# Output projection weights loaded at the start, and part of the first block's output projection moved into the last attention head

## The chip, the cores and the metric

The kernel runs on one core of a Trainium2 chip. The metric is device microseconds of one execution, the median of several runs. The core has a matrix engine (TensorE, PE in the profile, with its weight loads as PEld), VectorE (DVE), ScalarE (ACT), GpSimd (POOL) and the sync engine (SP), which here only issues transfers. 16 DMA engines move data. SBUF is the on-chip memory of 128 partitions, PSUM the memory that matrix products are written to.

## The reference

In short form, one layer with x of shape (1, 2048, 256): attention over 16 heads of 128, then a mixture of 8 experts of which 2 are used for each token. Weights of the attention come as codes and block scales (32 rows share a scale), and w = codes × scales.

```python
def attn(x):                                   # x: layernorm of the input
    q, k, v = (mxfp4(x, w) + b for w, b in ...)          # 256 -> 2048
    scores = einsum("bqhd,bkhd->bhqk", q, k) / sqrt(128)
    out = einsum("bhqk,bkhd->bqhd", softmax(scores), v)  # 2048 x 2048 per head
    return mxfp4(out, wo_codes, wo_scales) + bo          # 2048 -> 256
def ffn(x):                                    # x: layernorm of the sum so far
    top2 weights = normalised top 2 of softmax(x @ Wr)
    y_e = (silu(x @ Wg[e]) * (x @ Wu[e])) @ Wd[e]        # e = 0..7, I = 176
    return sum over e of weight_e * y_e
x = x + layernorm(attn(layernorm(x)))
x = x + layernorm(ffn(layernorm(x)))
```

## The kernel before

**Numbers.** For accuracy most products are made in two parts: a value is split into a high half in fp16 (or fp32r) and a low half that is the rest. Scores take three matmuls per tile (high×high, high×low, low×high), and so do the products with v.

**Stages.** A lead-in normalises x, transposes it (`xnT`) and makes the first projections. The main loop has 16 heads × 16 tiles of 128 queries, counted by g = 16 h + t, and two steps more (`NS` = 256, g = 256 and 257) that only finish softmax work. The tail does the output projection of four blocks of 512 queries, the two layernorms, the router and the experts.

**One step g of the main loop**, in the order in which each engine gets its instructions: scores of the first half of the keys into PSUM (12 matmuls for both halves, L492 to L496) and their maximum on DVE (L497); the second half of the low part of tile g−2 (`pl`, DVE, L537); a part of the products with v (`pv_unit`, L563); the high part of tile g−1 (`ph`, ACT, L522); scores of the second half, then exponentials on ACT (`p`, L508); the first half of `pl` of tile g−1. `ph` and `pl` are written as [queries, keys], and the products with v need [keys, queries]: each is transposed by a transfer on the sync queue (`pth` L525, `ptl` L543), two per step, 512 in all. The products with v run 13 units (6.5 steps) behind. Projections of the next head's q and k, and of v for the next pair of heads, fill the step (`fill`, L591); in head 15 only q is left, at t = 0, 4 and 8.

**Slots.** One pool of SBUF tiles (`kqv`, tag "x", `NX` = 21 slots of 4 KB per partition) holds `kT`, `v`, `ph`, `pl`, `wo`, the staging of weights, `oi` and other tiles of the tail. A new tile takes the slot that has been free for longest in the order of the program, and its writer waits until the last reader of the old tile is done; for `ph` and `pl` that includes the transposing transfer.

**Output of a head.** When a block of 512 queries of a head is done, ACT evicts the sum (`t32`, L578), POOL splits it (L579, L580) and stores it to DRAM (`ot_d`, L583). The output projection later loads it back in tiles `oi` of 4 heads × 256 queries, 512 KB each, on the sync queue (`load_oi`, L698). `op_mm(b, half, js)` adds up the products of 256 queries of block b with heads 4j to 4j+3, 16 matmuls a j, into one PSUM tile.

**Output weights.** `wo` is stored in DRAM as codes and scales. In head 14 three of its eight parts are loaded on POOL's queue (`load_wo_part`, L620), in head 15 five (`load_wo`, L637): each has four broadcast loads of scales on ACT's queue, L641, and one of codes on the sync queue, L646. POOL multiplies them (`dequant_wo`, L654, 128x512, eight times). With `wo` there, the row of biases is made (`bias_row`, `bias_row2`, L656 to L670), at t = 12 and 13 of head 15. `late(t)` (L718) also loads the gate weights (`wg`, t = 7 to 11), splits them (t = 10 to 13), and loads the first `oi` tiles (t = 9 and 11 to 14; three more at g = NS).

**Tail.** L1078 onwards: the last `pv` units (9, of which the first belongs to the last but one block), the output projection of block 0 (`op_pass(0, 0)`, `op_pass(0, 1)`, 128 matmuls), layernorms, router, and that of block 1 between them; then 44 steps of gate, up and down products with the rest in between.

The order of each engine's instructions is that of the program: nothing is rescheduled (`manual_schedule`). PSUM tiles of the projections have one buffer a tag ("pj", "pv"), scores have three ("s").

Of the kernel before, what the change touches and what calls it, by code (L numbers as in the profile page):

```python
# [37 lines left out]
def sandwich(  # L38
# [183 lines left out]
    def proj_qk(which, h, b, tag="pj", wide=None):  # L222
# [12 lines left out]
        t = kq_tile(which, h, b)  # L235
# [41 lines left out]

    with tc.tile_pool(name="start", bufs=4) as st:
# [18 lines left out]
        for i, (which, codes, scales) in enumerate(  # L297
            (("k", wk_codes, wk_scales), ("q", wq_codes, wq_scales), ("v", wv_codes, wv_scales))
        ):
            nc.gpsimd.dma_start(out=sc8[:, i], in_=scales[:, 0:256])  # L300
            cd = st.tile([128, 2, 256], F32, name="cd0", bufs=3)
            nc.sync.dma_start(
                out=cd, in_=codes.rearrange("(kc p) n -> p kc n", p=128)[:, :, 0:256]
            )
            cds[which] = (i, cd)
        nc.gpsimd.memset(one3, 1.0)
# [284 lines left out]
    def fill(h, t):  # L591
# [3 lines left out]
        if t in QK:  # L595
# [19 lines left out]
    wo = []  # L615
    so = wo_scales.rearrange("(h b) n -> b h n", b=4)
    co = wo_codes.rearrange("(h p) n -> p h n", p=128)
    wo_raw = {}

    def load_wo_part(j, part):  # L620
        hs = slice(2 * j, 2 * j + 2)
        if part == 0:
            wo_raw[j] = (
                stage.tile([128, 2, D], F32, name="wos", tag="st_s"),
                stage.tile([128, 2, D], F32, name="woc", tag="st_c"),
            )
        sc, cd = wo_raw[j]
        if part < 2:
            for b in (2 * part, 2 * part + 1):
                nc.gpsimd.dma_start(  # L630
                    out=sc[32 * b : 32 * b + 32],
                    in_=so[b : b + 1, hs].to_broadcast([32, 2, D]),
                )
        else:
            nc.gpsimd.dma_start(out=cd, in_=co[:, hs])

    def load_wo(j, pool, tags, bufs):  # L637
        hs = slice(2 * j, 2 * j + 2)
        sc = pool.tile([128, 2, D], F32, name="wos", tag=tags[0], bufs=bufs)
        for b in range(4):  # L640
            nc.scalar.dma_start(  # L641
                out=sc[32 * b : 32 * b + 32],
                in_=so[b : b + 1, hs].to_broadcast([32, 2, D]),
            )
        cd = pool.tile([128, 2, D], F32, name="woc", tag=tags[1], bufs=bufs)
        nc.sync.dma_start(out=cd, in_=co[:, hs])  # L646
        wo_raw[j] = (sc, cd)

    def dequant_wo(j):
        sc, cd = wo_raw.pop(j)  # L650
        if j % 4 == 0:
            wo.append(kqv.tile([128, 8, D], BF, name="wo", tag="x", bufs=NX))
        hs = slice(2 * (j % 4), 2 * (j % 4) + 2)
        nc.gpsimd.tensor_tensor(wo[j // 4][:, hs], cd, sc, ALU.mult)  # L654
# [12 lines left out]
    def bias_row2(b3):  # L667
        pb2 = psA.tile([128, 512], F32, name="pb2", tag="pj")
        nc.tensor.matmul(pb2[:, :D], one3, b3, start=True, stop=True)
        nc.vector.tensor_tensor(crow, pb2[:, :D], crow, ALU.add)  # L670
# [27 lines left out]
    def load_oi(b, half, j, tag="x"):  # L698
# [3 lines left out]
        nc.sync.dma_start(  # L702
# [9 lines left out]
    gw, crow = None, None  # L712
    gst = {}

    WO_LOAD = (0, 2, 4, 6, 8)
    WG_LOAD = (7, 9, 10, 11)

    def late(t):  # L718
        nonlocal gw, crow
        if t in WO_LOAD:  # L720
            load_wo(3 + WO_LOAD.index(t), kqv, ("x", "x"), NX)
        if t - 1 in WO_LOAD:
            dequant_wo(3 + WO_LOAD.index(t - 1))
        if t == 13:
            bias_row2(gst.pop("b3"))
        if t == 12:
            gst["b3"] = bias_row()
        if t == 9:
# [3 lines left out]
            crow = rp.tile([128, D], F32)  # L732
            nc.sync.dma_start(out=crow, in_=bo.partition_broadcast(128))
        if 10 <= t < 14:
            split_gu(gw, t - 10, gst.pop(t - 10), True)
        if t in WG_LOAD:
            i = WG_LOAD.index(t)
            gst[i] = load_gu(wg, i, kqv, "x", NX)
        if t == 9:
            load_oi(0, 1, 0, "x")  # L740
        if 11 <= t < 15:
            load_oi(0, 0, t - 11)

    X1 = {}
    XV = x.rearrange("b (c p t) d -> p (b c) t d", p=128, t=4)
# [3 lines left out]
    for g in range(NS + 2):  # L749
# [8 lines left out]
        if g == NS:  # L758
            load_oi(0, 1, 1)
            load_oi(0, 1, 2)  # L760
            load_oi(0, 1, 3)
# [35 lines left out]
        if h == NH - 2 and t in (8, 12):  # L797
            dequant_wo(t // 4 - 2)
        if h == NH - 1 and t == 0:
            dequant_wo(2)  # L800
        if h == NH - 2 and t >= 4 and t % 4 < 3:
            load_wo_part(t // 4 - 1, t % 4)
        if h == NH - 1:
            late(t)
        if g == NS:
            X1[0] = kqv.tile([128, 4, D], F32, name="x1_0", tag="x", bufs=NX)
            nc.sync.dma_start(out=X1[0], in_=XV[:, 0])
    UEND = 2 * (NS + 2)


    AT, MV, XT, CT = {}, {}, {}, {}

    OPS = {}

    def aux_psum(shape, dtype, name, tag):
        if tag == "s":
            return psS.tile(shape, dtype, name=name + "_s", tag="s", bufs=3)
        return psA.tile(shape, dtype, name=name, tag=tag)

    def op_mm(b, half, js, tag="pj"):  # L820
        if js[0] == 0:
            if half == 0:
                AT[b] = kqv.tile([128, 4, D], F32, name="at", tag="x", bufs=NX)
                MV[b] = small.tile([128, 4, 2], F32, name="mv")
            OPS[(b, half)] = aux_psum([128, 2, D], F32, "op", tag)
        ps = OPS[(b, half)]
        for j in js:
            oi = OIN.pop((b, half, j))
            for t in range(2):
                for hh in range(4):  # L830
                    for hl in range(2):
                        nc.tensor.matmul(  # L832
                            ps[:, t], oi[:, hh, hl, bass.ts(t, 128)],
                            wo[j // 2][:, 4 * (j % 2) + hh, :],
                            start=(j == 0 and t == 0 and hh == 0 and hl == 0),
                            stop=(j == 3 and t == 1 and hh == 3 and hl == 1),
                        )
        if js[-1] == 3:
            at = AT[b]
            tt = slice(2 * half, 2 * half + 2)  # L840
            nc.vector.scalar_tensor_tensor(
                at[:, tt], ps, sig[:, 0, 2:3],
                crow.unsqueeze(1).to_broadcast([128, 2, D]), ALU.mult, ALU.add,
            )
            stats(at, MV[b], 2 * half, 2 * half + 2)

    def op_pass(b, half, tag="pj"):
        op_mm(b, half, (0, 1, 2, 3), tag)

    def stats(src, mv, t0, t1):  # L850
        bs = small.tile([128, 4, 6], F32, name="bs")
        for t in range(t0, t1):
            nc.vector.bn_stats(bs[:, t], src[:, t, :])
        for t in range(t0, t1):
            nc.vector.bn_aggr(mv[:, t, :], bs[:, t])

    def norm(dst, src, mv, r):
        for t in range(4):
# [379 lines left out]
```

## Time and profile before

| what | value |
|---|---|
| runs | 1836.58 to 1838.99 us, median of 4: 1838.6 us |
| profiled execution | 1837.48 us, span 1835.7 us, granted clock 0.995 |
| TensorE busy | 1777.7 us, 97% of the span |
| DVE, ACT, POOL busy | 1626.8, 1369.8, 956.0 us |
| one step of the main loop | 5.86 to 5.90 us in heads 1 to 13, 5.94 in head 14, 6.17 in head 15 |
| end of the scores of head 15 | about 1544 us after the span's start |
| first gate product | 1602.58 us |

A step's time is the distance between the first `ph` of a head and that of the next, over 16. "Busy" counts an engine's own work. "Idle before" is the time in which an engine had nothing to do before an instruction, and the releaser is what it waited for last. The granted clock is the share of full speed at which TensorE was allowed to run. A DMA issue has a duration on its queue and, later, a landing.

### The profile page before, as it was taken

The page shows a single profiled execution, that of the slowest core. Times are in us where ns is not written, and L with a number is a line of the kernel's source. Part 1 is how long each engine was busy: PE and PEld are TensorE (multiplying, and loading weights), DVE is VectorE, ACT ScalarE, POOL GpSimd, SP SyncE. Part 2 cuts the span into 40 slices and gives each one's busy share as a digit, 9 for nine tenths or more (in the row PEclk, how much of TensorE's full clock was granted, in tenths as well). Part 3 has the DMA queues.
Part 4 walks back from the last instruction along what each step waited for, and adds up shares of the span by engine and source line. Part 5 has one row for each costly group of instructions (what it writes and reads, how often), then busy time and mean ns, then how long its engine had stood idle before and what let it go on. Part 6 is the DMA issues. An engine that isn't in the chain of part 4 may idle for free. (4 is left out here: it accounts for less than half of the span.)

```text
span 1835.7 us, 25522 instructions
## 1 busy us (share of the span) xinstructions
PE 1777.7 (97%) x8890; PEld 933.4 (51%) x8890; DVE 1626.8 (89%) x2267; ACT 1369.8 (75%) x1730; POOL 956.0 (52%) x929
## 2 busy tenths in 40 slices
PE   6899999999999999999999999999999988899998
PEld 4344444444444444444444444444444434688887
DVE  7999999999999999999999999999999886468566
ACT  5888888888888888888888888888888776222232
POOL 3366566555655565556565656565546433323232
PEclk9999999999999999999999999999999999999999
DMA  2999999999999999999999999999999999921000
GB/s 84 178 203 201 197 206 196 198 199 199 197 198 202 199 196 200 204 204 188 205 201 199 201 194 206 195 195 202 193 189 208 210 216 240 345 87 35 1 12 24
DMA packets 1091505, 330.71 MB, mean 180 GB/s; under 512 B 1070048, under 2 KB 1078064, under 8 KB 1091376
## 3 DMA queue, kind: packets, MB, share of 16 engines
q1 hardware_dynamic: 1078688, 298.14, 88.4%
q0 software_dynamic: 10544, 29.40, 5.9%
q10 hardware_dynamic: 2144, 1.54, 0.3%
q8 instruction: 70, 1.15, 0.2%
q14 instruction: 59, 0.48, 0.1%
HBM read 41.68 MB, written 18.87 MB: 33 GB/s over the span
## 5 line engine op out<-in xcount | busy, mean ns | idle before, releaser
L508 ACT ACTIVATE p<-s,m,ssc 128x1024 f32<-128x1024 f32 x512 | 612.1, 1199 | 183.7 <-DVE m L501 174.4
L537 DVE SCALAR_TENSOR_TENSOR pl<-p,m,ph 128x1024 f16<-128x1024 f32 x512 | 723.6, 1413 | 12.8 <-ACT ph L522 12.7
L497 DVE TENSOR_REDUCE m<-s 128x1 f32<-128x1024 f32 x512 | 622.1, 1215 | 28.0 <-PE s L496 26.2
L522 ACT ACTIVATE ph<-p,m 128x2048 f16<-128x2048 f32 x256 | 512.9, 2003 | 53.5 <-ACT t L274 14.5
L563 PE MATMUL pv<-pth,v 128*128 128x512 f16 x2048 | 507.8, 381 | 14.0 <-ACT p L508 5.3
L563 PEld LDWEIGHTS <-v 128*128 128x128 f16 x3072 | 301.0, 98 | 382.5 <-issue 11.7
L492 PE MATMUL s<-kT,qT 128*128 128x512 f16 x1024 | 388.7, 380 | 11.6 <-ACT p L508 10.7
L493 PE MATMUL s<-kT,qT 128*128 128x512 f16 x1024 | 388.5, 379 | 0.0
L496 PE MATMUL s<-kT,qT 128*128 128x512 f16 x1024 | 305.0, 379 | 0.0
L563 PE MATMUL pv<-ptl,v 128*128 128x512 f16 x1024 | 251.9, 379 | 0.0
L244 POOL CAST qT<-t 128x512 f16<-128x512 f32 x63 | 80.0, 1270 | 234.3 <-ACT t L243 234.3
L275 POOL CAST v<-t 128x256 f16<-128x256 f32 (+1 forms) x105 | 43.1, 410 | 255.4 <-ACT t L274 255.4
L276 POOL TENSOR_TENSOR v<-t,v 128x256 f16<-128x256 f32 (+1 forms) x105 | 163.8, 1560 | 8.5
L493 PEld LDWEIGHTS <-qT 128*128 128x128 f16 x1024 | 100.2, 98 | 125.2 <-issue 19.7
L496 PEld LDWEIGHTS <-qT 128*128 128x128 f16 x1024 | 100.3, 98 | 121.2 <-issue 0.6
L492 PEld LDWEIGHTS <-qT 128*128 128x128 f16 x1024 | 100.2, 98 | 110.0 <-issue 1.4
L993 POOL TENSOR_TENSOR hh<-sg,hh 128x512 fp32r<-128x512 f32 x42 | 55.1, 1312 | 143.3 <-ACT hh L992 108.7
L992 ACT CAST hh<-sg 128x512 fp32r<-128x512 f32 (+1 forms) x45 | 27.5, 611 | 107.1 <-DVE sg L1004 107.0
L580 POOL TENSOR_TENSOR o<-t,o 128x512 f16<-128x512 f32 x63 | 98.9, 1570 | 5.2
L508 ACT ACTIVATION_READ_ACCUMULATOR p<-s,m,ssc 128x1 f32 x512 | 99.0, 193 | 0.0
L244 POOL CAST kT<-t 128x512 f16<-128x512 f32 x60 | 65.5, 1091 | 55.9 <-ACT t L243 48.3
L245 POOL TENSOR_TENSOR kT<-t,kT 128x512 f16<-128x512 f32 x60 | 88.0, 1467 | 5.1
(186 smaller groups left out, 1831.7 us busy)
## 6 DMA issues: line engine op xcount, KB each, us to landing
oi<-ot_d SPq DMA_DIRECT2D x32, 512.0 KB, 5.5
ot_d<-o POOLq DMA_DIRECT2D x63, 256.0 KB, 4.5
pth<-ph SPq DMA_TRANSPOSE x256, 5.0
ptl<-pl SPq DMA_TRANSPOSE x256, 5.2
xt<-in_L_attn_x SPq DMA_DIRECT2D x4, 512.0 KB, 4.6
x<-in_L_attn_x SPq DMA_DIRECT2D x4, 512.0 KB, 6.2
st_s<-in_L_attn_wv_scales POOLq DMA_DIRECT2D x28, 64.0 KB, 4.2
st_c<-in_L_attn_wv_codes POOLq DMA_DIRECT2D x14, 128.0 KB, 4.3
```

The lines of the kernel that those rows point to most:

```text
L244: nc.gpsimd.tensor_copy(t[:, 0, :], t32)
L245: nc.gpsimd.tensor_tensor(t[:, 1, :], t32, t[:, 0, :], ALU.subtract)
L276: nc.gpsimd.tensor_tensor(v[:, 1, sl, :], t32, v[:, 0, sl, :], ALU.subtract)
L492: nc.tensor.matmul(s[:, j, :], q[:, 0, qc], k[:, 0, :], start=True, stop=False)
L493: nc.tensor.matmul(s[:, j, :], q[:, 0, qc], k[:, 1, :], start=False, stop=False)
L496: nc.tensor.matmul(s[:, j, :], q[:, 1, qc], k[:, 0, :], start=False, stop=True)
L497: nc.vector.tensor_reduce(m[:, half : half + 1], s, AX.XY, ALU.max)
L508: nc.scalar.activation(p[:, bass.ts(i, 1024)], s, AF.Exp, bias=m[:, 2:3], scale=ssc[:, 0:1], accum_out=m[:, 3 + i : 4 + i],)
L522: nc.scalar.activation(ph, p, AF.Copy, scale=m[:, 6:7])
L537: nc.vector.scalar_tensor_tensor(pl[:, cs], p[:, cs], m[:, 6:7], ph[:, cs], ALU.mult, ALU.subtract)
L563: nc.tensor.matmul(ps, V[(h // 2, c // 4)][:, i % 2, c % 4, dc], d[:, :, c, :], start=(n == 0), stop=(n == 47),)
L580: nc.gpsimd.tensor_tensor(o[:, :, 1, :], halves(t32), o[:, :, 0, :], ALU.subtract)
```

## The change

All codes and scales of `wo` are loaded in the lead-in, on the sync queue after the codes of the first projections, into eight slots of the pool: four loads of 512 KB and 16 of 128 KB. POOL multiplies them at g = 0 to 3, now as 128x1024, four times, and `wo`'s two tiles keep their two slots until the tail. `load_wo_part` and `load_wo` are gone, and with them every transfer that ACT issues after the lead-in.

In head 15 the three q projections come at t = 0, 1 and 2, two of them into slots of the pool (`qT_l`), so that the projections' memory is given up at t = 3 instead of 9. Head 14 gets `early(t)`: the bias row's load at t = 7, its products at t = 9 and 11, and an addition on POOL at 13, the `oi` tiles of block 0's first half for heads 0 to 11 at t = 8, 10 and 12, the first piece of `wg` at 14. `late(t)` in head 15 loads the rest of `wg` at t = 0, 3 and 5 and splits at t = 4, 6, 8 and 10, loads eight `oi` tiles (t = 2 to 14, three of them of block 1) and x of block 0 (t = 8).

`op_mm` of block 0 runs for heads 0 to 11 in head 15, first half at t = 4 to 6, second at t = 8 to 10. This sum is evicted by ACT and POOL adds the bias; heads 12 to 15 follow at t = 14 and 15 and are added on DVE. The first layernorm of block 0 is at g = NS and NS + 1, where the last `oi` tile of block 1's first half and all four pieces of `wu` are loaded too.

In the tail both of the first pieces of `wd` are loaded first; products of block 1 stand before the last `pv` units, then layernorm, transpositions, router; two of the four splits of `wu` go to DVE instead of POOL.

```diff
+        for q in range(4):
+            hs = slice(4 * q, 4 * q + 4)
+            wc = kqv.tile([128, 4, D], F32, name="woc", tag="x", bufs=NX)
+            nc.sync.dma_start(out=wc, in_=co[:, hs])
+            ws = kqv.tile([128, 4, D], F32, name="wos", tag="x", bufs=NX)
+            for b in range(4):
+                nc.sync.dma_start(
+                    out=ws[32 * b : 32 * b + 32],
+                    in_=so[b : b + 1, hs].to_broadcast([32, 4, D]),
+                )
+            wo_raw[q] = (ws, wc)
...
-        if t in QK:
+        if h == NH - 1:
+            if t < 3:
+                proj_qk("q", h, t + 1, wide=soft, slot="x" if t > 0 else None)
+        elif t in QK:
...
-    def load_wo_part(j, part):
...
-    def load_wo(j, pool, tags, bufs):
...
-    def dequant_wo(j):
-        sc, cd = wo_raw.pop(j)
-        if j % 4 == 0:
+    def dequant_wo(q):
+        sc, cd = wo_raw.pop(q)
+        if q % 2 == 0:
             wo.append(kqv.tile([128, 8, D], BF, name="wo", tag="x", bufs=NX))
-        hs = slice(2 * (j % 4), 2 * (j % 4) + 2)
-        nc.gpsimd.tensor_tensor(wo[j // 4][:, hs], cd, sc, ALU.mult)
+        hs = slice(4 * (q % 2), 4 * (q % 2) + 4)
+        nc.gpsimd.tensor_tensor(wo[q // 2][:, hs], cd, sc, ALU.mult)
...
-        nc.vector.tensor_tensor(crow, pb2[:, :D], crow, ALU.add)
+        nc.vector.tensor_copy(crow, pb2[:, :D])
...
-    WO_LOAD = (0, 2, 4, 6, 8)
-    WG_LOAD = (7, 9, 10, 11)
+    GW_LOAD = {0: 1, 3: 2, 5: 3}
+    GW_SPLIT = {4: 0, 6: 1, 8: 2, 10: 3}
+    OI_LOAD = {
+        2: (0, 1, 0), 4: (0, 1, 1), 6: (0, 1, 2), 9: (1, 0, 0), 10: (1, 0, 1),
+        12: (0, 0, 3), 13: (0, 1, 3), 14: (1, 0, 2),
+    }
+    OI_USE = {
+        4: (0, (0,)), 5: (0, (1,)), 6: (0, (2,)), 8: (1, (0,)), 9: (1, (1,)), 10: (1, (2,)),
+        14: (0, (3,)), 15: (1, (3,)),
+    }
...
+    def early(t):
+        nonlocal crow, brow
+        if t == 7:
+            cb = kqv.tile([128, 2, D], F32, name="crow", tag="x", bufs=NX)
+            crow, brow = cb[:, 0], cb[:, 1]
+            nc.sync.dma_start(out=brow, in_=bo.partition_broadcast(128))
+        if t == 9:
+            gst["b3"] = bias_row()
+        if t == 11:
+            bias_row2(gst.pop("b3"))
+        if t == 13:
+            nc.gpsimd.tensor_tensor(crow, crow, brow, ALU.add)
+        if t in (8, 10, 12):
+            load_oi(0, 0, t // 2 - 4)
+        if t == 14:
+            gst[0] = load_gu(wg, 0, kqv, "x", NX)
...
     def late(t):
+        if t == 3:
+            proj_ctx.close()
...
+        if t in OI_USE:
+            op_mm(0, *OI_USE[t], "pj", 2)
+        if t in GW_SPLIT:
+            split_gu(gw, GW_SPLIT[t], gst.pop(GW_SPLIT[t]), True)
+        if t in GW_LOAD:
+            i = GW_LOAD[t]
+            gst[i] = load_gu(wg, i, kqv, "x", NX)
+        if t in OI_LOAD:
+            load_oi(*OI_LOAD[t])
+        if t == 8:
+            X1[0] = kqv.tile([128, 4, D], F32, name="x1_0", tag="x", bufs=NX)
+            nc.sync.dma_start(out=X1[0], in_=XV[:, 0])
...
-        if js[-1] == 3:
+        if js[-1] == 3:
+            add = at[:, tt] if part == 2 else cb
+            nc.vector.scalar_tensor_tensor(
+                at[:, tt], ps, sig[:, 0, 2:3], add, ALU.mult, ALU.add,
+            )
+            stats(at, MV[b], 2 * half, 2 * half + 2)
+        elif js[-1] == part:
+            nc.scalar.activation(at[:, tt], ps, AF.Copy, scale=sig[:, 0, 2:3])
+            nc.gpsimd.tensor_tensor(at[:, tt], at[:, tt], cb, ALU.add)
...
+        if g < 4:
+            dequant_wo(g)
+        if h == NH - 2:
+            early(t)
         if h == NH - 1:
             late(t)
         if g == NS:
+            ln_a(0)
+        if g == NS + 1:
+            load_oi(1, 0, 3)
+            ust = [load_gu(wu, 0, kqv, "x", NX)]
+            ust += [load_gu(wu, i, kqv, "x", NX) for i in range(1, 4)]
+            ln_b1(0)
...
     pv_unit(UEND)
-    op_pass(0, 0, "s")
-    op_pass(0, 1, "s")
+    d0 = load_d(0)
+    d1 = load_d(4)
+    op_mm(1, 0, (0, 1), "s")
+    ln_b2(0)
+    split_gu(uw, 0, ust[0], True)
+    ln_c(0)
+    for e in range(1, 5):
+        pv_unit(UEND + e)
+    tr(0, 0, "s")
+    tr(0, 1, "s")
+    split_gu(uw, 1, ust[1], False)
+    op_mm(1, 0, (2, 3), "s")
+    for j in range(4):
+        load_oi(1, 1, j)
+    router_a(0, "s")
+    for e in range(5, 7):
+        pv_unit(UEND + e)
+    split_gu(uw, 2, ust[2], True)
+    router_b(0, "s")
+    split_gu(uw, 3, ust[3], False)
+    for e in range(7, 9):
+        pv_unit(UEND + e)
...
+    op_mm(1, 1, (0, 1), "s")
     router_d(0, "s")
-    d1 = load_d(4)
-    split_d(*d0)
     split_d(*d1)
-    op_mm(1, 1, (0, 1, 2, 3), "s")
+    op_mm(1, 1, (2, 3), "s")
```

## The prediction

> **What bounds the kernel now.** I read the page first, then busy time by stretch, then the waits and the timeline of the stretch that falls off. Durations come from one profiled execution: 1837.48 us, of which 1835.7 are span. It lies 1.1 us under the median of the runs shown (1838.6), so a forecast for the profile is raised by 1.1.
>
> The page: TensorE is busy in 97% of the span, so little but its gaps can be won. The fifth line below is the sync engine's DMA queue: the transpositions of `ph` and `pl` keep the 16 DMA engines 88% busy. There are two resources without slack, not one.
>
> ```profile
> span 1835.7 us, 25522 instructions
> PE 1777.7 (97%) x8890; PEld 933.4 (51%) x8890; DVE 1626.8 (89%) x2267; ACT 1369.8 (75%) x1730; POOL 956.0 (52%) x929
> PE   6899999999999999999999999999999988899998
> DMA  2999999999999999999999999999999999921000
> q1 hardware_dynamic: 1078688, 298.14, 88.4%
> ```
>
> By stretch (columns: PE, PEld, DVE, ACT and POOL busy us with counts, granted clock, DMA share, GB/s): TensorE is full up to 1450 us, and short by 6.0, 8.3 and 6.1 us in the three stretches after it, head 15 and the tail. The clock drops to 0.90 there, and the DMA engines stay at a share above 1. So this stretch waits for DMA.
>
> ```profile
> 1400.00:1450.00 50.00, 50.00 (x231) 22.32 (x230) 46.73 (x61) 40.94 (x51) 27.61 (x27) 1.00 1.11 204
> 1450.00:1500.00 50.00, 43.97 (x201) 19.43 (x199) 43.26 (x56) 37.56 (x44) 18.65 (x17) 1.00 1.14 218
> 1500.00:1550.00 50.00, 41.71 (x183) 18.12 (x182) 36.90 (x50) 37.67 (x43) 17.77 (x12) 0.90 1.06 229
> 1550.00:1600.00 50.00, 43.85 (x315) 30.55 (x314) 20.46 (x59) 14.03 (x16) 14.69 (x11) 0.97 1.07 316
> 1600.00:1650.00 50.00, 49.41 (x335) 42.90 (x334) 29.96 (x60) 10.52 (x18) 17.11 (x12) 1.00 0.35 131
> ```
>
> The timeline shows how (start, duration, engine, [idle before, releaser]). A transposition that normally occupies the sync queue for about 2.9 us takes 6.17 us behind three `oi` loads; the last `pth` is therefore issued only at 1565.17 and TensorE waits 3.29 us for it. Then come a wait for `oi` (1.80), one for the router (0.92), and the first gate product at 1602.58. From there on TensorE is full. Earlier, `ph` on ACT waits 3.78 us for a slot or a queue and TensorE 3.00 us with it.
>
> ```profile
> 1502.74 2.00 ACT L522 ACTIVATE ph<-p,m 128x2048 f16<-128x2048 f32 x1 [3.78 <-DMA gu_raw<-in_L_ffn_Wg]
> 1505.98 0.59 PE L492 MATMUL s<-kT,qT 128*128 128x512 f16 x1 [3.00 <-ACT p L508]
> ...
> 1558.91 6.17 SPq L543 DMA_TRANSPOSE ptl<-pl  x1
> 1565.17 2.94 SPq L525 DMA_TRANSPOSE pth<-ph  x1
> 1570.39 1.89 PE L563 MATMUL pv<-pth,v 128*128 128x512 f16 x4 [3.29 <-DMA pth<-ph]
> ...
> 1579.20 3.67 PE L832 MATMUL op_s<-wo,oi 128*128 128x256 bf16 x32 [1.80 <-DMA oi<-ot_d]
> ...
> 1595.18 0.66 PE L963 MATMUL pct_s<-ident,cx 128*128 128x128 f32 x4 [0.92 <-DVE cx L951]
> ...
> 1602.58 0.71 PE L978 MATMUL gup<-xT,gw 128*128 128x512 f32 x2
> ```
>
> TensorE's gaps from 1450 to 1600 add up to 20.3 us; matmuls after a gap run at 0.43 us instead of 0.215, some 5 us more. At most about 25 us can be won here.
>
> **The change, part by part.** TensorE's matmuls are the same in number and shape; only their order changes.
>
> *Lead-in.* 4 `woc` and 16 `wos` loads, 4 MB, go on the sync queue after the codes. That queue has nothing to issue between about 8.4 and 41.5 us, and 20 issues at about 0.45 us (the 0.38 to 0.57 of `oi` and `gu_raw` rows) end near 18 us. The first slice of the span shows the DMA engines at 2 tenths. Cost 0; if the loads delay the last `x` piece, up to 2.
>
> *Four dequantizations of 128x1024 on POOL at g = 0 to 3.* The rows are the 128x512 ones, 1.26 us alone, so some 2.5 us each; POOL has idle stretches of 8 us there. DVE is the bound of these iterations (TensorE waits 9.1 us in 5 times for `v`), and it collides with POOL: `pl` takes 1.27 us here and 2.28 at most, under a POOL operation with two inputs.
>
> ```profile
> PE pj L255 <- DVE v L267: 9.1, 5, 2.1
> L654 POOL TENSOR_TENSOR wo<-woc,wos x8: 1257/1272/2246, 1404.7 to 1508.7; 128x512 bf16<-128x512 f32 x8
> L537 DVE SCALAR_TENSOR_TENSOR pl<-p,m,ph x512: 1264/1416/2283, 41.5 to 1552.9; 128x1024 f16<-128x1024 f32 x171
> ```
>
> Four times 1.0 is the upper end, 0 the lower (a reduction from PSUM beside it shows no lengthening). I take +1: of DVE's 6.4 us per iteration 2.5 are `pl`, so a collision is partial as a rule. The Trainium skill ("SBUF — State Buffer", section on the two separate sides) says that the port pair of the two engines is an exclusive lock, and that the one that comes second is blocked for the whole instruction of the other. By it the sum would be four full blocks of 2.5, +10; the rows show both slowed and neither blocked throughout (a dequantization at 1404.69 kept its 1.26 us beside a `pl` of 1.97).
>
> *Two slots fewer (19 of 21) from then on.* A slot comes back to `ph` or `pl` after 3 to 4 iterations instead of 4 to 5, that is after 17 us or more; landings come 5 to 9 us after the write. Cost 0; a steady loss of 0.02 us in each of 220 iterations would be 4.
>
> *Head 14.* Bias products (1.9 + 0.7 us of TensorE) come here, where TensorE has no gap: between 0 and +2.6. I take +1. ACT gets no new wait: the copy of `b3` is short.
>
> *DMA traffic ahead of the last `pth`.* Before, in heads 14 and 15: `wos`/`woc` 1.57 + 2.62 MB, `wg` 1.44, bias 0.13, eight `oi` 4.19, together 9.95. After: eleven `oi` 5.77, `wg` 1.44, `x1_0` 0.52, bias 0.13, together 7.86. That is 2.1 MB less on engines that are full. Copies alone ran 8.8 MB in 24 us (1574 to 1598), near 0.4 MB/us, so −5.3. Among transpositions they ran slower: 1557.05 to 1565.17 less one transposition of 2.9 for three `oi`, 0.3 MB/us, so −7. Lower end: head 14's 1.57 MB, on the POOL queue, moved the iteration only from 5.88 to 5.94 us, 1 us in the head. If they were free, 0.5 MB count, −1.3. I take −5.3, between the ends and with the larger body of rows. The Trainium skill ("DMA: Bandwidth & Descriptors", section on issuing engines that are not separate queues) says all queues run on the same 16 DMA engines and only issue time differs. By it the whole 2.1 MB count; by the row alone the sum is 4 us worse.
>
> *No DMA issued by ACT.* The `wos` issues stood in ACT's stream and waited for transpositions; that is a part of the 20.3 us of gaps. It frees TensorE, but the next to end last is the landing of `pth` again, so I count nothing beyond it.
>
> *Products of block 0.* The 128 matmuls at 1552.56 to 1567.10 (14.5 us) move into head 15 (96 at t = 4 to 10, 32 at t = 14, 15). They stand today in front of the wait for the last `pth`, so they are covered by it already; taken into head 15 they stay covered, as long as TensorE reaches that wait before the landing. Its work up to there would end at 1567.1 − 14.3 (gaps) − 5 (slow clock) + 3.7 = 1552, against a landing near 1565. Nothing gained, nothing lost; ACT's two evictions (0.6 each) and DVE's 0.75 + 1 twice lie in engines with over 10 us of idle per 50.
>
> *The tail after the landing.* 128 products stood behind it, now 96, since (1,0,(0,1)) go ahead of it: −3.7 (the row at 1579.20). The router gap of 0.92 has 12 `pv` and 32 products above it now: −0.9. The `oi` wait of 1.80: three of four tiles are loaded in head 15, but the next four follow `wu` and `wd` on the same queue; half, −0.9. Together −5.5.
>
> Sum: −5.3 − 5.5 + 1 + 1 = −8.8; 1837.5 becomes 1828.7, and as a median about 1829.
>
> **The rivals.** *A, slower: slots in head 15.* `oi`, `x1_0`, `at` and two `qT_l` now take slots there, and by the order in which the pool hands out its slots eight `ph` reuse one that was `ph` or `pl` two iterations earlier, three right on a `pl` whose transposition was issued one iteration before. ACT then stands until it lands, and everything behind it: `p`, the scores, and the next transposition, so that the DMA engines run dry. Like waits cost TensorE 1.31, 1.54, 1.63, 1.07 and 3.00 us in head 15 of before, mean 1.7. Eight make +13.7, with the other terms +4.9; at 3.0 each +24, so +15: 1843 to 1854, I say 1846. Against it: two transpositions of 2.9 us stand behind the awaited one, more than the 2.0 us of `ph`. It decides from 1.1 us a time on (8.8 / 8).
> *B, no change: the start.* Dequantizations at +1 a collision and the last `x` late by 2, plus head 14's full 2.6 and only −1.3 for the traffic: 4 + 2 + 2.6 − 1.3 − 5.5 = +1.8, about 1840.
> *C, more.* At the slowest rate seen among transpositions (1511.10 to 1519.32 less one: 1.0 MB in 5.3 us) 2.1 MB are −11; with the whole tail (−6.4) and no charges −17: 1821.
>
> **How the numbers follow.** Own case 0.54 (range 1824 to 1835: −7 and −1.3 for the traffic, no charge or both full), A 0.28, C 0.12, B 0.06. 0.2%, 3.7 us, is about what a measurement of this kernel can tell from no change. Faster 0.66, same 0.06, slower 0.28. The range is 1818 to 1847: it leaves out A's dearer half and a little of C.
>
> **What would show it.** Last `pth` landing near 1565 + 2 (charges) instead of 1570.34; first gate product near 1594; head 15's iterations above 6.2 us, with `op` rows filling old gaps; no wait of POOL on `woc` (32.2 us now). Wrong if ACT's `ph` rows in head 15 show waits on `pth`/`ptl` of over 1.1 us eight times; if the DMA share from 1450 to 1570 falls under 1.0; or if `pl` at 40 to 70 us is over 2 us and the sixth iteration starts late.

## The result and the profile after

The changed kernel takes 1843.0 us (median of 39 runs, 1837.61 to 1846.44), the kernel before 1838.8 us (60 runs). The ratio is 1.002, 95% interval 1.0015 to 1.0025: 3.7 us slower, between 2.8 and 4.6. Forecast were 1829 us and a gain. Ratios and intervals leave out one of the ten executions of e4 below, which took 2665 us at a granted clock of 0.66 instead of 0.99.

The page of the changed kernel: the counts of matmuls are the same, and TensorE's busy time differs by 1.1 us. The second slice of the TensorE line has fallen from 8 to 6 tenths.

```profile
span 1841.8 us, 25510 instructions
PE 1778.8 (97%) x8890; PEld 935.0 (51%) x8890; DVE 1637.7 (89%) x2269; ACT 1371.0 (74%) x1732; POOL 943.3 (51%) x911
PE   6699999999999999999999999999999989899997
q1 hardware_dynamic: 1081744, 301.02, 89.6%
```

By stretch, with the columns as in the forecast; first one row of the kernel before, then the changed kernel. Between 50 and 100 us TensorE is now busy for 36.09 us at clock 0.89, before for 41.71 at 1.00.

```profile
50.00:100.00 50.00, 41.71 (x204) 19.44 (x202) 47.42 (x64) 41.93 (x54) 22.72 (x29) 1.00 0.98 180
```

```profile
50.00:100.00 50.00, 36.09 (x162) 16.54 (x160) 43.74 (x51) 33.05 (x42) 17.09 (x15) 0.89 0.80 145
1400.00:1450.00 50.00, 48.79 (x236) 22.45 (x235) 45.00 (x58) 39.78 (x49) 19.65 (x19) 1.00 1.08 202
1450.00:1500.00 50.00, 43.88 (x209) 20.75 (x208) 38.27 (x50) 36.14 (x44) 15.74 (x13) 0.93 1.11 209
1500.00:1550.00 50.00, 50.00 (x266) 25.78 (x264) 42.60 (x56) 39.95 (x46) 17.14 (x11) 1.00 1.14 223
1550.00:1600.00 50.00, 42.56 (x250) 24.26 (x248) 33.08 (x74) 24.52 (x29) 12.91 (x10) 0.97 1.06 267
```

From 1500 to 1550 us TensorE is now full: the products of block 0 fill what were gaps. Where the time went is best seen in five marks of the two traces (us from the start of the span; e1 is the first experiment below).

| mark | before | after | difference | e1 |
|---|---|---|---|---|
| first product with v | 71.94 | 84.63 | +12.7 | 71.40 |
| first `ph` of head 15 | 1450.89 | 1463.58 | +12.7 | 1449.96 |
| last `pth` landed | 1570.34 | 1580.05 | +9.7 | 1563.54 |
| first gate product | 1602.58 | 1605.81 | +3.2 | 1589.04 |
| last gate product begins | 1822.81 | 1826.04 | +3.2 | 1809.32 |

So 12.7 us are lost before step 6, nothing more up to head 15, 3.0 are won up to the last landing and 6.5 from there to the first gate product. The span grew by 6.1 and not by 3.2, because it ends 6.5 us after the last DVE instruction instead of 3.5. What holds the end is a DRAIN, an instruction that POOL executes after its last operation (count; shortest, median and longest in ns; first and last start; before, then after):

```profile
L1234 POOLq DRAIN  x3: 46/166/1562, 1829.5 to 1835.4; - x3
```

```profile
L1235 POOLq DRAIN  x3: 98/194/7932, 1832.7 to 1841.4; - x3
```

The longest takes 7.93 us instead of 1.56. It does so in all ten kernels of this document that have the early weights, e2 among them, which has nothing else of the change; in the three without them (before, e9, e10) it is 1.56. What about the early weights sets it, no run separates.

The timeline of the changed kernel from 41 us on (start, duration, engine, operation, [idle before, releaser]) shows the loss itself:

```profile
41.03 2.36 POOL L642 TENSOR_TENSOR wo<-woc,wos 128x1024 bf16<-128x1024 f32 x1
41.09 3.38 DVE L556 SCALAR_TENSOR_TENSOR pl<-p,m,ph 128x1024 f16<-128x1024 f32 x1 [0.16 <-ACT ph L541]
...
45.08 2.36 POOL L642 TENSOR_TENSOR wo<-woc,wos 128x1024 bf16<-128x1024 f32 x1
...
45.84 2.69 DVE L556 SCALAR_TENSOR_TENSOR pl<-p,m,ph 128x1024 f16<-128x1024 f32 x1
...
56.34 7.21 DVE L556 SCALAR_TENSOR_TENSOR pl<-p,m,ph 128x1024 f16<-128x1024 f32 x1
...
57.81 4.65 POOL L642 TENSOR_TENSOR wo<-woc,wos 128x1024 bf16<-128x1024 f32 x2
```

`pl` takes 1.27 us alone. Here it ends at 44.47, 48.53 and 63.55, that is 1.08, 1.09 and 1.09 us after the end of the multiplication beside it (43.39, 47.44, 62.46), whenever it began. It does not run slowly; it stands still until POOL is done. The three take 9.5 us more than alone. The third, with 5.9 of these, is only in part explained: it began 1.47 us ahead of its multiplications, beside three transfers that POOL issues, and alone it would have been done 0.2 us before they began. DVE sets the pace in these steps, so TensorE waits for each (view of the waits, 30 to 85 us: waited for, us in total, times, longest; before, the first line had 9.1 us, as the forecast shows):

```profile
PE pj L258 <- DVE v L270: 18.6, 5, 8.1
ACT p L527 <- DVE m L520: 14.4, 5, 7.2
```

After its gaps of 5.4 and 8.1 us TensorE also runs slowly for a while: from 29 us to the first product with v, 14 matmuls begin 0.3 to 0.7 us after the one before instead of 0.215, which adds 2.9 us (before: one, 0.3 us). 9.5 and 2.6 add up to 12.1 of the 12.7.

### The profile page after: what moved, and what is told of

The parts are those of the page before. It is cut to its first block, busy times and chain, and to the rows that moved or that the text cites. A ratio compares the mean times of both kernels' runs of the same rounds, so it can differ in the third digit from the quotient of the medians.

```text
span 1841.8 us, 25510 instructions
## 1 busy us (share of the span) xinstructions
PE 1778.8 (97%) x8890; PEld 935.0 (51%) x8890; DVE 1637.7 (89%) x2269; ACT 1371.0 (74%) x1732; POOL 943.3 (51%) x911
## 5 line engine op out<-in xcount | busy, mean ns | idle before, releaser
L556 DVE SCALAR_TENSOR_TENSOR pl<-p,m,ph 128x1024 f16<-128x1024 f32 x512 | 732.6, 1431 | 12.5 <-DMA pth<-ph 5.0
L511 PE MATMUL s<-kT,qT 128*128 128x512 f16 x992 | 377.4, 380 | 8.0 <-ACT p L527 7.3
L512 PE MATMUL s<-kT,qT 128*128 128x512 f16 x992 | 377.4, 380 | 0.0
L515 PE MATMUL s<-kT,qT 128*128 128x512 f16 x992 | 295.6, 380 | 0.0
L515 PEld LDWEIGHTS <-qT 128*128 128x128 f16 x992 | 97.3, 98 | 118.0 <-issue 1.6
L512 PEld LDWEIGHTS <-qT 128*128 128x128 f16 x992 | 97.2, 98 | 116.4 <-issue 14.4
L511 PEld LDWEIGHTS <-qT 128*128 128x128 f16 x992 | 97.3, 98 | 106.2 <-issue 1.9
L599 POOL TENSOR_TENSOR o<-t,o 128x512 f16<-128x512 f32 x63 | 93.6, 1485 | 5.2
L258 PE MATMUL pj<-wv,xnT 128*128 128x256 bf16 x512 | 75.9, 277 | 18.7 <-DVE v L270 18.6
```

The lines of the kernel that those rows point to most:

```text
L511: nc.tensor.matmul(s[:, j, :], q[:, 0, qc], k[:, 0, :], start=True, stop=False)
L512: nc.tensor.matmul(s[:, j, :], q[:, 0, qc], k[:, 1, :], start=False, stop=False)
L515: nc.tensor.matmul(s[:, j, :], q[:, 1, qc], k[:, 0, :], start=False, stop=True)
L556: nc.vector.scalar_tensor_tensor(pl[:, cs], p[:, cs], m[:, 6:7], ph[:, cs], ALU.mult, ALU.subtract)
L599: nc.gpsimd.tensor_tensor(o[:, :, 1, :], halves(t32), o[:, :, 0, :], ALU.subtract)
```

## The experiments

Ratios are to the kernel before, run on the same chip, with 95% intervals; 0.001 is 1.84 us.

**e1: the multiplications ahead of the main loop.**

```diff
-        if g < 4:
-            dequant_wo(g)
...
+    for q in range(4):
+        dequant_wo(q)
     for g in range(NS + 2):
```

> The changed kernel with the four output-weight multiplications issued on POOL before the main loop, where POOL stands idle from about 26 to 39 us, instead of at g = 0 to 3. Theory (the start's 12.7 us come from POOL's two-input operation keeping DVE's `pl` from its data while DVE is the bound): the three stretched `pl` of the changed kernel (3.38, 2.69 and a sum of 7.21 us) go back to 1.27, the first `pv` product comes back from 84.6 us to about 72, and the time falls by 12 us against the changed kernel: 8 to 9 us below the kernel before. Rival (the 4 MB of loads in the lead-in, or the eight slots they hold, cost the time): the first `pv` product stays near 84 us and the time stays 3 to 4 us above the kernel before.

Measured: 1830.42 us, ratio 0.996 (0.9945 to 0.9974), 7.4 us below the kernel before. The timeline of e1: the four multiplications fill POOL's idle time, the last one's data having landed at about 33 us, and `pl` is back at 1.27.

```profile
26.28 9.28 POOL L642 TENSOR_TENSOR wo<-woc,wos 128x1024 bf16<-128x1024 f32 x4
...
40.96 1.28 DVE L556 SCALAR_TENSOR_TENSOR pl<-p,m,ph 128x1024 f16<-128x1024 f32 x1 [0.17 <-ACT ph L541]
43.73 1.27 DVE L556 SCALAR_TENSOR_TENSOR pl<-p,m,ph 128x1024 f16<-128x1024 f32 x1
```

The first product with v comes at 71.40. (The profiled execution is the shortest of its five runs, 1826.94 us, 3.5 us under their median; marks of e1 carry that much doubt.) Loads, kept tiles and staging slots are all still there, so up to this mark they cost nothing; the whole loss there came from when the multiplications run. This version is faster than both kernels, although POOL's DRAIN at the end takes 7.93 us in it too.

**e2: the early weights alone, in the kernel before.**

```diff
+        for q in range(4):
...
+            nc.sync.dma_start(out=wc, in_=co[:, hs])
...
+            for b in range(4):
+                nc.sync.dma_start(
+                    out=ws[32 * b : 32 * b + 32],
+                    in_=so[b : b + 1, hs].to_broadcast([32, 4, D]),
+                )
+            wo_raw[q] = (ws, wc)
...
-        if t in WO_LOAD:
-            load_wo(3 + WO_LOAD.index(t), kqv, ("x", "x"), NX)
-        if t - 1 in WO_LOAD:
-            dequant_wo(3 + WO_LOAD.index(t - 1))
...
-        if h == NH - 2 and t in (8, 12):
-            dequant_wo(t // 4 - 2)
-        if h == NH - 1 and t == 0:
-            dequant_wo(2)
-        if h == NH - 2 and t >= 4 and t % 4 < 3:
-            load_wo_part(t // 4 - 1, t % 4)
+        if g < 4:
+            dequant_wo(g)
```

> The kernel before with one part of the change alone: output weights loaded in the lead-in and multiplied at g = 0 to 3 on POOL, as in the changed kernel; everything in heads 14 and 15 and in the tail as before, without the weight loads there. Theory (the loss sits at the start): first `pv` product near 84.6 us, +12.7; heads 14 and 15 lose 4.2 MB of traffic, at 0.3 to 0.4 MB/us 10 to 14 us earlier landing of the last transposition if that is what they wait for, so that the sum is within 3 us of the kernel before. Rival (the loss comes from the products and tile slots newly in head 15, rather than from the start): the start is not late, and the time is over 5 us below the kernel before.

Measured: 1842.26 us, ratio 1.0028 (1.0016 to 1.0039), 5.1 us slower. The first product with v is at 81.43, 9.5 late rather than 12.7, with `pl` rows of 3.39, 2.68 and 3.96 us. The last `pth` lands at 1570.05, 0.3 us earlier than before: heads 14 and 15 do win the start's 9.5 us back, at the low end of what was expected, and no more. The sum lies outside the 3 us that the theory gave, on the slow side; the rival, a start without loss, is out. In the profile the first gate product comes 0.9 us later than before, within the theory's 3 us, and 2.5 of the 3.5 us that its span is longer lie behind the last DVE instruction, with POOL's DRAIN. In heads 14 and 15 of this run TensorE's waits on ACT's `p` are six, each under 0.32 us: the gaps of 1 to 3 us of before went with the weight loads there. That ACT's part of them was the reason is not separated from those on POOL and on sync.

**e3: the multiplications at g = 8 to 11.**

```diff
-        if g < 4:
-            dequant_wo(g)
+        if 8 <= g < 12:
+            dequant_wo(g - 8)
```

> The changed kernel with the four multiplications on POOL at g = 8 to 11, after the v projections that DVE finishes at g = 0 to 5. Theory (POOL stretches `pl` anywhere, and it costs time where DVE sets the pace): the `pl` rows beside them are still stretched to 2.5 us or more, but TensorE is the bound there and DVE has 2 to 3 us of idle per 50, so a part of each stretch is hidden: 4 to 10 us below the changed kernel, 0 to 6 below the kernel before. Rival (loads or held slots): staged tiles hold their eight slots for eight steps longer, so the loss is the same or larger, 3 us or more above the kernel before.

Measured: 1834.92 us, ratio 0.9986 (0.9977 to 0.9996), 2.6 us below the kernel before. `pl` is stretched here too (3.35 and 3.68 us beside two of the four, 1.93 and 1.70 beside the others), 5.6 us in all instead of 9.5, and head 1 starts 4.5 us late instead of 12.6. A microsecond of wait thus cost 0.8 us here and 1.3 at the start. The shorter waits are a part of the difference; that DVE's slack is the rest is the theory, not shown by itself.

**e4: the multiplications on DVE itself.**

```diff
-        nc.gpsimd.tensor_tensor(wo[q // 2][:, hs], cd, sc, ALU.mult)
+        nc.vector.tensor_tensor(wo[q // 2][:, hs], cd, sc, ALU.mult)
```

> The changed kernel with the four multiplications at g = 0 to 3 moved from POOL to DVE itself. Theory (POOL blocks DVE for the whole of its 2.36 us): DVE needs about 1.3 us for each (its row for `pl` of the same size), so although the busiest engine gets more work, the start is shorter: about 5 us late instead of 12.7, 6 to 8 us below the changed kernel. Rival (DVE is merely the bound there and its own load decides): +5 us or more on top of the changed kernel.

Measured: 1834.41 us (nine executions), ratio 0.998 (0.9966 to 0.9994); the first product with v is 2.5 us late. DVE needs 1.22 to 1.23 us for each. Giving the busiest engine the work is cheaper than leaving it beside, on POOL.

**e5: most of the products of block 0 left out of head 15 of e1.**

```diff
+            few = b == 0 and j < 3
+            nh, nl = (1, 1) if few else (4, 2)
             for t in range(2):
-                for hh in range(4):
-                    for hl in range(2):
+                for hh in range(nh):
+                    for hl in range(nl):
```

> The kernel of e1 with 84 of the 96 products of block 0 for heads 0 to 11 left out of head 15 (two matmuls per `oi` tile instead of 16, so the tiles are still loaded, read and given back at the same places; the result of block 0 then lacks these heads' rest). It takes 84 x 0.115 = 9.7 us of TensorE work out of head 15. Theory (the end of head 15 is set by the transpositions on the sync queue, and the products stand in time that TensorE would wait for the last `pth` anyway; it waits 5.7 us there in e1): the last `pth` lands within 2 us of e1's 1563.5, the wait before it grows by most of 9.7, the time stays within 2.5 us of e1. Rival (TensorE's load in head 15 sets the end; the products are paid for): landing and time come 6 to 10 us earlier than in e1.

Measured: 1827.71 us, ratio 0.9935 (0.9916 to 0.9955). Against the ratio of e1 that is 4.6 us less, with intervals that overlap. In the profile, counted from the first product with v (73.88 here, a later start than in e1), the last `pth` lands 1.9 us and the first gate product comes 1.1 us earlier than in e1. The wait ahead of the last `pth` did not grow, as the theory had it: it is 4.9 us, and TensorE's new gaps stand earlier, in waits for `p` and for `oi` (3.3 us). So by the medians about half of the 9.7 us of products is paid for, between what the theory and the rival gave, and in the profile 1 to 2 us; the intervals allow from nothing to all of it. That they are free is not shown.

**e6: three `oi` loads moved behind the last `pth`.**

```diff
     OI_LOAD = {
-        2: (0, 1, 0), 4: (0, 1, 1), 6: (0, 1, 2), 9: (1, 0, 0), 10: (1, 0, 1),
-        12: (0, 0, 3), 13: (0, 1, 3), 14: (1, 0, 2),
+        2: (0, 1, 0), 4: (0, 1, 1), 6: (0, 1, 2),
+        12: (0, 0, 3), 13: (0, 1, 3),
     }
...
-            load_oi(1, 0, 3)
+            for j in range(4):
+                load_oi(1, 0, j)
...
-    op_mm(1, 0, (0, 1), "s")
     ln_b2(0)
...
         pv_unit(UEND + e)
+    op_mm(1, 0, (0, 1), "s")
     tr(0, 0, "s")
```

> The kernel of e1 with three `oi` loads (block 1, first half; 1.57 MB) moved from head 15 to behind the last `pth`, at g = 257, and the 32 products that use the first two moved behind the first four `pv` units of the tail. Theory (the landing of the last `pth` goes by the bytes ahead of it, at 0.3 to 0.4 MB/us): it lands 3.9 to 5.2 us earlier than in e1; 3.7 us of products are behind it instead of ahead, so the time is 0 to 1.5 us below e1, or up to 3 above if the `oi` tiles come late for their products. Rival (the landing goes by when the softmax writes `ph`, not by the bytes): it moves by less than 2 us and the time is 2 us or more above e1.

Measured: 1831.64 us, ratio 0.9961 (0.9947 to 0.9975), the same as e1. From the first `ph` of head 15 to the last landing it takes 111.3 us, 113.6 in e1: 2.3 us for 1.57 MB, about half of what the theory gave, though more than the rival's 2. From that landing to the first gate product it takes 29.2 instead of 25.5 us, 3.7 more, which is the length of the 32 products. Products behind the last landing count in full. For the bytes ahead of it, the 2.3 us are half of what their transfer time would give. But the profiles of the six kernels with the same head 15 (the changed kernel, e1, e3, e4, e8, e11) already differ by more: the stretch is 112.9 to 116.5 us in them. The theory's price is not confirmed, and no effect of these bytes is shown.

**e7: 20 slots instead of 21, in e1.**

```diff
-NX = 21
+NX = 20
```

> The kernel of e1 with 20 slots in the pool instead of 21. Theory (waits of ACT's `ph` for a slot in head 15 are there, but the transpositions queued on sync cover them, so that they shift no end): more or longer `ph` waits on `pth` or `ptl`, and a time within 3 us of e1. Rival (slot reuse sets the pace of head 15, rival A of the prediction): a step there is longer by 0.3 us or more and the time 4 us or more above e1.

Measured: 1832.94 us, ratio 0.9961 (0.9946 to 0.9977), as e1. In its profile, though, a step of head 15 takes 7.08 us (6.68 in e1, 6.68 to 6.89 in the six kernels named above) and the last `pth` lands 119.9 us after the head's first `ph` (113.6). A step is here the distance from the head's first `ph` to its last over 15; the 6.17 us given above for before divides these 15 steps by 16, and 6.58 is right. The times speak for the theory, the profile for the rival; the profiled execution is the longest of its four runs (1837.94 us), and that of e1 the shortest of its five, so the marks of the two cannot be set against each other. How near head 15 is to being limited by slots stays open.

**e8: POOL's transfers after the multiplication within a step of the changed kernel.**

```diff
+        if g < 4:
+            dequant_wo(g)
         if live:
             weight_steps(h, t)
         if h == 0 and t in (8, 9):
             tail_consts(t - 8)
-        if g < 4:
-            dequant_wo(g)
```

> The changed kernel with POOL's multiplication ahead of its weight loads within the steps g = 0 to 3. In the changed kernel one `pl` took 7.21 us; two multiplications in a row explain 4.65 us of wait, and the 1.3 us before them lie beside three transfers that POOL issues. Theory 1 (only the multiplications hold DVE's `pl` back): `pl` beside issues alone stays at 1.27, and each stretched `pl` ends 1.1 us after the multiplication beside it; the sum of the stretches is 7 to 10 us again. Theory 2 (the issues hold it back too): a `pl` beside issues without a multiplication is stretched by 0.5 us or more.

Measured: one run of 1835.06 us; the first product with v is 5.3 us late, and the stretches sum up to 4.2 us instead of the 7 to 10 expected. The timeline of e8 shows why the price is not fixed:

```profile
54.71 1.63 DVE L556 SCALAR_TENSOR_TENSOR pl<-p,m,ph 128x1024 f16<-128x1024 f32 x1
55.22 3.33 POOL L642 TENSOR_TENSOR wo<-woc,wos 128x1024 bf16<-128x1024 f32 x1
58.38 1.28 DVE L556 SCALAR_TENSOR_TENSOR pl<-p,m,ph 128x1024 f16<-128x1024 f32 x1
58.49 0.58 POOL L132 DMA_DIRECT2D st_s<-in_L_attn_wv_scales  x1
59.07 1.16 POOL L138 DMA_DIRECT2D st_c<-in_L_attn_wv_codes  x2
60.24 2.36 POOL L642 TENSOR_TENSOR wo<-woc,wos 128x1024 bf16<-128x1024 f32 x1
61.32 2.37 DVE L556 SCALAR_TENSOR_TENSOR pl<-p,m,ph 128x1024 f16<-128x1024 f32 x1
```

At 55.22 `pl` had begun first (itself 0.4 us late behind the POOL operation before), and it is POOL that waits: 3.33 us instead of 2.36. At 60.24 POOL was first and `pl` waits. Beside transfers alone (58.38) `pl` is not stretched, which speaks for theory 1. Against it stand a `pl` of 1.67 us beside transfers alone in e11, at 54.50, which is 0.4 over and so under theory 2's 0.5, and the 1.5 us that the `pl` of 7.21 us stood before its multiplications began. Whether POOL's issuing can hold `pl` back stays open.

**e9 and e10: POOL work that has nothing to do with the change, in the kernel before.** Two constant tiles are multiplied into a third at the same four places (e9); in e10 the third is filled with zeros instead, twice.

```diff
+    xa = kqv.tile([128, 4, D], F32, name="xa", tag="x", bufs=NX)
+    xb = kqv.tile([128, 4, D], F32, name="xb", tag="x", bufs=NX)
+    xo = kqv.tile([128, 4, D], F32, name="xo", tag="x", bufs=NX)
+    nc.gpsimd.memset(xa, 1.0)
+    nc.gpsimd.memset(xb, 1.0)
     for g in range(NS + 2):
...
+        if g < 4:
+            nc.gpsimd.tensor_tensor(xo, xa, xb, ALU.mult)
```

> The kernel before, with nothing of the change: four idle POOL multiplications of 128x1024 from two constant tiles are added at the end of the steps g = 0 to 3 (same engine, places and size as the changed kernel's, fp32 out; no loads, no weights kept, three slots of the pool for these steps). Theory (POOL reading two inputs keeps DVE's `pl` off for its whole length, and that alone is the start's loss): `pl` rows of 2 to 4 us and more beside them, the first `pv` product 5 to 13 us later than in the kernel before (e8 showed that the amount goes by where the four fall), and a time 4 to 12 us above it. Rival (the lead-in's loads or the tiles kept are needed for the loss): first `pv` within 2 us, time within 3 us of before.

> As e9, with two POOL fills of 128x1024 with zeros, which read no tile, in place of each multiplication. Theory (what collides is POOL's reading, as the notes on the port pair say of a DVE operation with two inputs): `pl` beside the fills stays at 1.27 us and the time within 3 us of the kernel before. Rival (any POOL operation that uses the on-chip memory holds DVE off): `pl` rows of 2 us and more and a time 4 us or more above before.

Measured: e9 1847.03 us, ratio 1.0042 (1.0025 to 1.0059), 7.7 us slower, first product with v 10.2 us late; e10 1839.13 us, ratio 1.0002 (0.9993 to 1.0012), first product with v 0.4 us early. The timelines, e9 first:

```profile
40.93 2.35 POOL L803 TENSOR_TENSOR xo<-xa,xb 128x1024 f32<-128x1024 f32 x1
40.98 3.38 DVE L537 SCALAR_TENSOR_TENSOR pl<-p,m,ph 128x1024 f16<-128x1024 f32 x1 [0.17 <-ACT ph L522]
```

```profile
41.05 1.96 POOL L804 MEMSET xo<- 128x1024 f32 x2
41.12 1.28 DVE L537 SCALAR_TENSOR_TENSOR pl<-p,m,ph 128x1024 f16<-128x1024 f32 x1 [0.17 <-ACT ph L522]
```

With no load, no weight and no new order the loss is there; with a POOL operation that only writes it is not. That a fill is shorter (0.95 us) is not the reason: in e11 pieces of 0.72 us that read do hold `pl` up. What `pl` waits for is a POOL operation that reads.

**e11: each multiplication in four pieces.**

```diff
-        nc.gpsimd.tensor_tensor(wo[q // 2][:, hs], cd, sc, ALU.mult)
+        for i in range(4):
+            w = wo[q // 2][:, 4 * (q % 2) + i]
+            nc.gpsimd.tensor_tensor(w, cd[:, i], sc[:, i], ALU.mult)
```

> The changed kernel with each of the four multiplications cut into four pieces of 128x256, one after the other at the same places. Theory (the length of one POOL operation is what DVE waits for, and DVE goes in between two): no `pl` is stretched by more than about 0.7 us, the first `pv` product is 2 to 5 us later than in the kernel before, and the time is 6 to 10 us below the changed kernel. Rival (POOL's next operation takes its turn before DVE's waiting one, as in the two in a row that `pl` waited out for 4.65 us): the stretches and the time stay as in the changed kernel.

Measured: 1834.17 us, ratio 0.9981 (0.9966 to 0.9996), by the ratios 7.2 us below the changed kernel. No `pl` beside the pieces or their transfers is over 1.85 us (0.58 more than alone), the six stretches add up to 2.7 us, and the first product with v is 0.8 us late, better than expected. POOL's piece that follows a waiting `pl` takes 1.70 instead of 0.72 us: DVE gets its turn between two pieces, and POOL then waits. The four multiplications are the same work at the same place; cut up, they cost 0.8 us at the start instead of 12.7, so the loss was the length of each.

## Why the prediction was wrong

Step by step, in the terms of its sum:

| step | forecast | measured |
|---|---|---|
| loads in the lead-in | 0 | 0: the first scores begin 0.4 us earlier, though the last load is issued at 28.4 us and not near 18 |
| four multiplications on POOL | +1 | +12.7 up to the first product with v |
| two slots fewer | 0 | 0 up to the first `ph` of head 14 (+12.2 there, +12.7 at the start) |
| head 14 | +1 | +0.5 |
| traffic ahead of the last `pth` | −5.3 | −3.0 (−3.0 to −6.5, mean −4.9, in the six kernels with this head 15) |
| products of block 0 | 0 | a part may be paid for (e5) |
| tail after the landing | −5.5 | −6.5 (e1: −6.7) |
| POOL's DRAIN at the end | not in the sum | +2.9 |

The differences in the last column are those between marks: head 14 and head 15 by their first `ph`, the landing from there (119.5 us before, 116.5 after, 113.6 in e1), the tail from the landing (32.2, 25.8, 25.5).

**The step that failed is "four times 1.0 is the upper end … I take +1".** Its mechanism, a collision of `pl` with POOL where DVE is the bound, was named and its size was wrong by a factor of twelve. Two readings were at fault.

First, the rows of 128x512 multiplications were taken as two engines that slow each other, by about 1.0 us a collision. They show turns. These two rows of the kernel before are the pair that the forecast quoted as proof that neither is blocked throughout:

```profile
1404.69 1.26 POOL L654 TENSOR_TENSOR wo<-woc,wos 128x512 bf16<-128x512 f32 x1
```

```profile
1405.06 1.97 DVE L537 SCALAR_TENSOR_TENSOR pl<-p,m,ph 128x1024 f16<-128x1024 f32 x1
```

POOL was first, ran its 1.26 us, and ended at 1405.95; `pl` ended at 1407.03, 1.08 us after that, the same 1.08 as in the changed kernel. The two other pairs of this kind in that trace, at 1470.08 and 1495.33 us, end 1.08 us apart as well. The 1.0 was thus no price of a collision, but about what was left of a POOL operation of 1.26 us when `pl` came. With operations of 2.36 us it grows with them, and two in a row made 4.65. An upper end from rows is only one if the row has the same size; that the new operation was twice as long stood in the same paragraph.

Second, the charge was cut from four to one because only 2.5 of DVE's 6.4 us per step are `pl`. But the meeting was not rare: POOL's first two multiplications begin 0.06 and 0.76 us ahead of a `pl` (41.03 and 41.09, 45.08 and 45.84), and a `pl` stood through the other two. On an engine without slack every wait also goes on to ACT and TensorE, and TensorE's slow matmuls after the gaps came on top. The forecast also called TensorE full up to 1450 us, although its own line of waits has 9.1 us for `v` here and the row from 50 to 100 us of before shows it short by 8.3.

The Trainium skill's rule that was weighed there ("SBUF — State Buffer", section on the two separate sides: an exclusive lock for the whole instruction) gave +10, and the rows as I read them +1. The runs side with the page: 9.5 us of waiting, +12.7 at the first product. Its section on who interferes with whom also says that a DVE operation with two inputs in SBUF contends with a GpSimd operation that reads there and not with one that only writes; e9 and e10 agree (+7.7 us and +0.4 of 1838). The `pl` that began 1.47 us ahead of its multiplications and still waited for both does not follow from the lock.

The term that the sum did not have, POOL's DRAIN, is the second part of the miss: 2.9 us of the profile's 6.1. Without it the profile would still be 3.2 us slower than before.

**Rival B** had the place (the start) and about a third of the price (4 of 12.7 us for the multiplications), so its sum stayed at +1.8. **Rival A** gave 1843 to 1854 us, and the measured 1843.0 agrees with its lower end by luck, since its cause was seen without deciding: ACT's `ph` waits for landings of `ptl` and `pth` in head 15, TensorE has one gap of 5.05 us for it, and the view of the waits from 1440 to 1610 us has

```profile
ACT ph L541 <- DMA ptl<-pl: 8.6, 2, 7.8
PE pv L582 <- issue: 5.4, 1, 5.4
```

Head 15's own end is 4.6 us later than at its start, relative to before (last `ph` +17.3 against +12.7), but behind it TensorE still waits 5.4 us for the last `pth`. That wait was forecast: with TensorE there first, the landing set the end. In the timeline of the changed kernel it is the product that begins right after the landing at 1580.05:

```profile
1573.80 2.71 SPq L544 DMA_TRANSPOSE pth<-ph  x1
...
1580.14 6.93 PE L582 MATMUL pv<-pth,v 128*128 128x512 f16 x24 [5.45 <-issue]
...
1605.81 1.63 PE L989 MATMUL gup<-xT,gw 128*128 128x512 f32 x6
```

**What was right.** Everything from the first product with v to the first gate product: −9.5 us measured (−3.0 and −6.5) against −9.8 forecast (1 − 5.3 − 5.5). With the start mended, e1 lies 7.4 us below the kernel before; without the 2.9 us at its end that would be 10.3, close to these 9.8. (The forecast's 1829 us left out the 1.1 us that it had named for the step from profile to median; with them its sum gives 1830.) Within these terms the price of the traffic is the least settled: e6 took 1.57 MB away and the landing came 2.3 us earlier, where 0.3 to 0.4 MB/us would give 3.9 to 5.2. How much of the landing hangs on bytes and how much on when the softmax writes the last `ph`, the runs do not say.

## What to carry to other kernels

When a row shows an operation longer than alone beside another engine, add up the ends before calling it a slowdown: if the longer one ends a fixed time after the other's end, it waited its turn, and the price grows with the length of the other operation. Put long two-input POOL operations where DVE has slack, or before the loop, or cut them into short pieces; moving work to an "idle" POOL is not free where DVE sets the pace. And a bound taken from rows has to be scaled to the size of the new operation before it is called an upper end.

## What the runs showed of the hardware that was not expected

Two POOL multiplications one after the other let a waiting `pl` in between in some places (e8, e9, and three of four in e11) and not in others: in the changed kernel `pl` stood through both (4.65 us), and in e2 it stood through the rest of one and the next as well. What decides the turn is open. A POOL fill of 128x1024, 0.95 us, beside `pl` changes neither. And the same four operations cost 5.3 or 12.7 us at the start, in one profile each, depending only on whether POOL's transfers of a step are issued after or before them. The end of the span, last, waited for a POOL DRAIN of 7.93 us in every kernel with the early weights, an instruction that the timeline does not list.
